# Delta rule, MLP and gated unit on one core: weight loads on another queue, other steps for the next pair's normalization

## The chip, the cores and the metric

The kernel runs on one core of a Trainium2 chip. The core's engines are TensorE (PE; its weight loads are shown as PEld), VectorE (DVE), ScalarE (ACT), GpSimd (POOL) and SyncE (SP, which here only issues DMAs). Each works through its own instructions in order and waits on semaphores for the others. The metric is the device time of one execution in microseconds, the median of several runs. Times inside an execution come from one profiled execution and count from the start of its span.

## The reference

The input is 32 sequences of 512 tokens with 256 features. Cut to what matters:

```python
def delta(x, gates_w, gates_b, lr_w, lr_b, out_w, out_b):
    q, k, v = split(x @ gates_w + gates_b, 3);  lr = x @ lr_w + lr_b
    k = k / norm(k)
    A = tril(k @ k.T, -1) + eye(T)
    u = solve_triangular(A, v, lower=True)
    return ((q @ k.T) @ (lr * u)) @ out_w + out_b

h = layernorm(x)                       # no gain, no offset
h = h + delta(layernorm(h) * dn_g + dn_b)
h = h + relu((layernorm(h) * mn_g + mn_b) @ w1 + b1) @ w2 + b2
x = x + h
n = layernorm(x)
return x + (silu(n @ w_gate.T) * (n @ w_up.T)) @ w_down.T    # integer weights times 1/127
```

## The kernel before

Sequences are worked on in 16 pairs. A sequence is four chunks of 128 tokens (partitions) by 256 features, one tile `a` of 128x1024 floats out of six. The engines' orders are the orders in which the Python program emits instructions: the schedule is written out by hand, with generators that are advanced at chosen places.

**The opening.** `load_a` puts the first sequence on SP's queue. `Gates` loads the weights of q, k, v and lr in three cuts (`CUTS`, the k part first, in its constructor; the others in `load_rest`) by `load`, four to eight DMAs a cut, and DVE and PE later fold the normalization's gain and offset into them (`fold`, `keys`, `rest`). `load_rest` also loads `out_w` and `out_b`. Then SP loads the second pair's sequences and `w1`, `w2`, and ACT's queue `b1`, `b2`, `mn_g`, `mn_b`. Only then does the program emit `normalized` of the first sequence, which needs DVE (statistics), ACT (L527, subtracting the mean with a row sum) and POOL (L415, a power for the reciprocal root), and PE's first transposes after it. All DMAs of ACT and SP share eight landing semaphores in turn; an issue that takes one over waits until the DMA that had it before has landed.

**One pair.** For pair g, whose predecessor is `old` and successor `following`, the loop emits: `middle` (the MLP of `old`, and the first steps of the triangular solve of pair g); the gated stage `gated(old)`, 84 steps of one product of a weight block and 256 columns each, two matmuls; and `values_phase` (contractions of pair g, down projections of `old`). In the gated stage, unit n of 12 takes seven steps p1 to p7; ACT copies PE's results out of PSUM (L1021, L1029, L1041), DVE adds and multiplies (L1075, L1070, L1059), POOL does further products (L1047, L1048, L1053, L1071) and the sums of the second sequence's input (L979, from step `MIX` on). Beside these the loop emits by step number i: solution steps (every third i until it is done), a store at `STORE`, loads of the following pair at `LOAD` and `TURN + 1`, the second sequence's normalization from `NORM` and its fetch at `TURN`, and from `EARLY` on the next pair's keys (`keys`: `pk`, L588) and Gram blocks (`gram`: `pg`, L617), which need the next pair's normalized sequences `ag`.

**The next pair's normalization.** `prepare(following)` runs `normalized` for both sequences of the next pair, one after the other. At i == `START` it is made a `Side`: every emitted product calls `spend(columns)`, which adds `columns * weight / cols` to what the side owes (a gated step spends 256, `keys` 1024, `gram` up to 1024), and `run` emits pieces of the generator as long as something is owed. A piece costs what it yields, 1 if it yields nothing. The pieces are: four statistics (`stats`, L409 and L410), the sums `vv`, `rr`, `nm` (L514 to L522), four activations (L527), `left`, `both`, `r2` with the first scaling (L533 to L543), three more scalings (L543), two small copies (L548, L549), four transposes of 32x32 blocks on DVE (L484), the sending of the transposed chunks to DRAM (L491, four DMAs on SP) and their fetch as `ag` (L497, SP).

```python
def run(self, cols):
    self.owed += cols * self.rate
    while self.owed > 0.0 and not self.over:
        w = next(self.gen, self)
        self.over = w is self
        self.owed -= 1.0 if w is None or self.over else w
```

The functions around the change, with the profile's line numbers:

Of the kernel before, what the change touches and what calls it, by code (L numbers as in the profile page):

```python
# [15 lines left out]
P = 128  # L16
# [6 lines left out]
def kernel(  # L23
# [40 lines left out]
    LEAD = 16  # L64
    NS = 2

    LOAD, NORM, STORE, TURN, START, MIX, EARLY = 1, 3, 8, 15, 16, 28, 56
    BEGIN = 17
    PREPARE = 13 * 1024
    INVERT = 17 * 1024  # L70
    INVERT_FIRST = 15 * 1024

# [91 lines left out]
    def by_feature(src, name, queue):  # L164
        t = const.tile([P, src.shape[0] // P], F32, tag=name, name=name)
        queue.dma_start(t, src.rearrange("(c p) -> p c", p=P))
        return t
# [24 lines left out]
    class Gates:  # L192


        def __init__(self, gw):

            self.gw = gw
            self.gb = wk.tile([1, GC], F32, tag="feat", name="gb", bufs=4)
            self.wlast = wk.tile([P, GC], F32, tag="feat", name="wlast", bufs=4)
            self.wt = [wk.tile([P, GC], F32, tag="dp", name=f"wt{f}") for f in range(NF)]  # L200
            self.load(*CUTS[0])
            self.dnb = by_feature(dn_b, "dnb", nc.sync)
            self.dng = by_feature(dn_g, "dng", nc.sync)
            self.glast = const.tile([P, 1], F32, name="glast")
            nc.sync.dma_start(self.glast, dn_g[C - 1 : C].partition_broadcast(P))
            self.put = wk.tile([P, NF, P], F32, tag="rhs", name="put", bufs=4)
            nc.gpsimd.memset(self.put, 0.0)
            nc.gpsimd.tensor_copy(self.put[:, :, LAST:P], self.dnb.unsqueeze(2))

        def load(self, lo_, hi_):  # L210
            top = min(hi_, 3 * C)
            for f in range(NF):
                nc.scalar.dma_start(
                    self.gw[f][:, lo_:top], gates_w[f * P : (f + 1) * P, lo_:top]
                )
            nc.scalar.dma_start(self.gb[:, lo_:top], gates_b[lo_:top].unsqueeze(0))
            nc.scalar.dma_start(
                self.wlast[:, lo_:top], gates_w[C - 1, lo_:top].partition_broadcast(P)
            )
            if hi_ > top:  # L220
                for f in range(NF):
                    nc.scalar.dma_start(self.gw[f][:, top:hi_], lr_w[f * P : (f + 1) * P, :])
                nc.scalar.dma_start(self.gb[:, top:hi_], lr_b.unsqueeze(0))
                nc.scalar.dma_start(
                    self.wlast[:, top:hi_], lr_w[C - 1].partition_broadcast(P)
                )

# [76 lines left out]
            nc.scalar.copy(wl, pl)  # L304

        def load_rest(self):
            self.load(*CUTS[1])
            self.load(*CUTS[2])
            self.room = wk.tile([P, NH, NF, C], F32, tag="hid", name="room")
            self.rooms = 0  # L310
            self.ow = self.scratch("ow")
            nc.scalar.dma_start(self.ow, out_w.rearrange("(c p) o -> p c o", p=P))
            self.obs = wk.tile([P, C], F32, tag="rhs", name="obs", bufs=4)
            nc.scalar.dma_start(self.obs, out_b.partition_broadcast(P))

# [86 lines left out]
    def stats(src, tag):  # L404

        st = small.tile([P, NT, nc.vector.BN_STATS_DIM], F32, tag="bnst", name=f"bnst_{tag}")
        mv = small.tile([P, NT, nc.vector.BN_AGGR_DIM], F32, tag="bnmv", name=f"bnmv_{tag}")
        for c in range(NT):
            nc.vector.bn_stats(st[:, c, :], src[:, c, :])  # L409
            nc.vector.bn_aggr(mv[:, c, :], st[:, c, :])  # L410
            yield
        return mv

    def rsqrt(dst, src):
# [92 lines left out]
    def normalized(s):  # L507

        n = s.n
        mv = yield from stats(s.a, f"a{n}")  # L510


        vv = small.tile([P, 2, NT], F32, tag="vv", name=f"vv_{n}")
        nc.vector.tensor_scalar(vv[:, 0, :], mv[:, :, 1], EPS, None, ALU.add)  # L514
        nc.vector.scalar_tensor_tensor(
            out=vv[:, 1, :], in0=vv[:, 0, :], scalar=EPS, in1=mv[:, :, 1],
            op0=ALU.mult, op1=ALU.add,
        )
        rr = small.tile([P, 2, NT], F32, tag="rr", name=f"rr_{n}")
        rsqrt(rr.rearrange("p a t -> p (a t)"), vv.rearrange("p a t -> p (a t)"))  # L520
        nm = small.tile([P, NT], F32, tag="nm", name=f"nm_{n}")
        nc.vector.tensor_scalar(nm, mv[:, :, 0], -1.0, None, ALU.mult)  # L522
        yield 8

        left = small.tile([P, NT], F32, tag="left", name=f"left_{n}")
        for c in range(NT):
            nc.scalar.activation(  # L527
                s.a[:, c, :], s.a[:, c, :], AF.Identity, bias=nm[:, c : c + 1], scale=1.0,
                accum_out=left[:, c : c + 1],
            )  # L530
            yield 2
        yield 8
        nc.vector.tensor_scalar(left, left, 1.0 / C, None, ALU.mult)  # L533

        both = small.tile([P, NT], F32, tag="both", name=f"both_{n}")
        nc.vector.tensor_tensor(both, rr[:, 0, :], rr[:, 1, :], ALU.mult)
        s.r2 = small.tile([P, 2, NT], F32, tag="r2", name=f"r2_{n}", bufs=5)
        nc.vector.tensor_tensor(
            s.r2, vv, both.unsqueeze(1).to_broadcast([P, 2, NT]), ALU.mult
        )  # L540
        s.hlast = small.tile([P, NT, 1], F32, tag="hlast", name=f"hlast_{n}", bufs=5)
        for c in range(NT):
            nc.vector.tensor_scalar(  # L543
                s.a[:, c, :], s.a[:, c, :], left[:, c : c + 1], rr[:, 0, c : c + 1],
                ALU.subtract, ALU.mult,
            )
            yield 2
        nc.vector.tensor_copy(s.hlast, s.a[:, :, C - 1 : C])  # L548
        nc.vector.tensor_copy(s.a[:, :, C - 1 : C], s.r2[:, 1, :].unsqueeze(2))  # L549
        yield  # L550
        if n // NS == 1:
            s.ag = wk.tile([P, NF, T], F32, tag="aT", name=f"ag_{n}")
        else:
            s.ag = wk.tile([P, NF, T], F32, tag="feat", name=f"ag_{n}", bufs=4)
        if n >= 2 * NS:
            t = Turn(f"a{n}")
            for c in range(NT):
                t.chunk(s.a[:, c, :], c)
                yield
            t.send()  # L560
            for _ in range(4):
                yield
            t.fetch(s.ag)
        yield
# [666 lines left out]

    whole = lambda gen: [None for _ in gen]

    def middle(old, rest, sides_, sol):

        one, two = old
        combined = iter([d.combined for d in rest[2:]])
        more = lambda *between: next(combined, lambda *b: [f() for f in b])(*between)
        step = lambda: rest and next(sol, None)
        more()  # L1240
        mlp_in(one, 0)
        step()
        norm = normed_steps(two, "m")
        next(norm)
        next(norm)
        mlp_in(one, 1)
        step()
        whole(norm)
        turned(two, "m")
        residual(one)  # L1250
        if rest:
            sides_[0].finish()
        mlp_out(one, 0, step)
        mlp_out(one, 1)
        step()
        if rest:
            normed(one, "f")
        for d in rest[:2]:
            d.store()
        more(step)  # L1260
        mlp_in(two, 0)
        residual(two)
        mlp_in(two, 1)
        if not rest:
            normed(one, "f")
        step()
        mlp_out(two, 0)
        step()
        turned(one, "f")
        whole(mixed(one))  # L1270
        mlp_out(two, 1)
        step()
        if not rest:
            next(sides_[0].gen)
            sides_[0].finish()
# [160 lines left out]
    with tc.manual_schedule(engines={  # L1436
# [24 lines left out]
            load_a(s)  # L1461
        w1s = matrix(w1, "w1s")
        w2s = matrix(w2, "w2s")
        b1s = by_feature(b1, "b1s", nc.scalar)
        b2s = const.tile([P, C], F32, name="b2s")
        nc.scalar.dma_start(b2s, b2.partition_broadcast(P))
        mng = by_feature(mn_g, "mng", nc.scalar)
        mnb = by_feature(mn_b, "mnb", nc.scalar)
        for _ in normalized(first[0]):
            pass  # L1470
        to_keys(first[0])
# [19 lines left out]
        for g in range(n_pairs):  # L1491
# [5 lines left out]
                rest = []  # L1497
            else:
                sol = solution(new)
                middle(old, rest, sides_, sol)  # L1500
                prep = None
                solved = False
                early = iter(())
# [8 lines left out]
                for i, _ in enumerate(gated(old)):  # L1512
# [6 lines left out]
                    if i == STORE:  # L1519
                        for d in rest[2:]:  # L1520
                            d.store()
                    if following and i == LOAD:
                        load_a(following[0])
                    if following and i == TURN + 1:
                        load_a(following[1])
                    if i == NORM:
# [7 lines left out]
                    if i >= MIX and i % 2 == 0:  # L1534
                        next(mix, None)
                    if i == START and following:
                        prep = Side(prepare(following), 2 * 50, PREPARE)
                for _ in sol:
                    pass
                if prep:  # L1540
# [52 lines left out]
```

## Time and profile before

| | |
|---|---|
| runs | 2088.59, 2092.3, 2093.04 us; median 2092.3 |
| profiled execution | 2088.74 us, span 2086.6 us |
| busy | PE 1983.9 us (95%), DVE 1350.9 (65%), ACT 918.3 (44%), POOL 1113.1 (53%) |
| DMA | 164.12 MB, 160.29 on SP's queue (q1), 1.71 on ACT's (q10) |
| gated stages | the first starts at 163.4 us, the others 124 to 127 us apart (the first pair 140) |

In the profile, a line `start length engine Lnn operation out<-in` is one group of instructions in the timeline, with the idle time of the engine before it and what ended it in brackets. `ACTq` and `SPq` are what the engines' sequencers issue, DMAs above all. A view of waits lists who waited for whom, with the total, the number of times and the longest. PE's busy time contains the pipelining of matmuls: two that follow each other 0.215 us apart show 0.38 us each.

### The profile page before, as it was taken

The page shows a single profiled execution, that of the slowest core. Times are in us where ns is not written, and L with a number is a line of the kernel's source. Part 1 is how long each engine was busy: PE and PEld are TensorE (multiplying, and loading weights), DVE is VectorE, ACT ScalarE, POOL GpSimd, SP SyncE. Part 2 cuts the span into 40 slices and gives each one's busy share as a digit, 9 for nine tenths or more (in the row PEclk, how much of TensorE's full clock was granted, in tenths as well). Part 3 has the DMA queues.
Part 4 walks back from the last instruction along what each step waited for, and adds up shares of the span by engine and source line. Part 5 has one row for each costly group of instructions (what it writes and reads, how often), then busy time and mean ns, then how long its engine had stood idle before and what let it go on. Part 6 is the DMA issues. An engine that isn't in the chain of part 4 may idle for free.

```text
span 2086.6 us, 31085 instructions
## 1 busy us (share of the span) xinstructions
PE 1983.9 (95%) x10286; PEld 1585.7 (76%) x10286; DVE 1350.9 (65%) x3788; ACT 918.3 (44%) x2499; POOL 1113.1 (53%) x1317
## 2 busy tenths in 40 slices
PE   5888999999999999999999999999999999999998
PEld 2566786878878787786878878787786878778887
DVE  3747484875849577484875749577584866748252
ACT  3335335353443535435353443635345353543543
POOL 2524364754645465464754646465464645546568
PEclk9799999999999999999999999999999999999999
DMA  3211132332423223232332423224142332323120
GB/s 89 64 54 28 44 103 78 81 108 60 116 64 99 82 60 108 57 105 77 80 108 61 115 64 99 82 61 121 44 130 61 86 107 60 103 64 90 51 61 21
DMA packets 248344, 164.12 MB, mean 79 GB/s; under 512 B 80849, under 2 KB 223832, under 8 KB 248184
## 3 DMA queue, kind: packets, MB, share of 16 engines
q1 hardware_dynamic: 244992, 160.29, 28.0%
q10 hardware_dynamic: 3112, 1.71, 0.3%
q8 instruction: 82, 1.34, 0.3%
q14 instruction: 78, 0.64, 0.1%
q0 software_dynamic: 80, 0.14, 0.0%
HBM read 96.02 MB, written 66.06 MB: 78 GB/s over the span
## 4 chain that ended last, share of the span: by engine, by line
PE 62%; DVE 16%; DMA 10%; ACT 4%; issue 3%; POOL 2%; SPq 2%; POOLq 0%; ACTq 0%; DVEq 0%
PE pg L617 7%; PE pk L588 5%; PE po_y L1134 5%; PE pyup L1007 5%; PE po_d L876 4%; PE pygate L1007 4%; PE pa L951 4%; PE po_x L1134 4%; PE pf L835 3%; PE pzgate L1007 3%; PE po_m L876 3%; PE pzup L1007 3%; PE pr L814 3%; DVE a L543 2%; DMA ag<-way_a 2%
## 5 line engine op out<-in xcount | busy, mean ns | idle before, releaser
L1070 DVE TENSOR_TENSOR top_up<-top_up,pzup 128x512 f32<-128x512 f32 x96 | 65.5, 682 | 223.4 <-PE pzup L1007 221.0
L1047 POOL TENSOR_TENSOR v_up<-v_up,five_up 128x256 f32<-128x256 f32 x96 | 69.9, 728 | 253.4 <-ACT v_up L1021 252.0
L1134 PEld LDWEIGHTS po_y<-wdS,hid 128*128 128x128 f32 x1536 | 179.7, 192 | 4.1 <-issue 1.0
L1134 PE MATMUL po_y<-wdS,hid 128*128 128x128 f32 x1536 | 182.8, 276 | 0.0
L1007 PE MATMUL pygate<-hS,wgS 128*128 128x256 f32 x576 | 173.7, 383 | 3.1 <-ACT top_gate L1041 2.5
L1007 PE MATMUL pyup<-hS,wuS 128*128 128x256 f32 x576 | 174.1, 384 | 1.9
L617 PE MATMUL pg<-kT 128*128 128x256 f32 (+3 forms) x512 | 159.3, 437 | 1.9 <-ACT kT L595 1.9
L1075 DVE TENSOR_TENSOR hid<-top_gate,pzgate 128x512 f32<-128x512 f32 x96 | 65.0, 677 | 143.1 <-PE pzgate L1007 143.0
L1134 PEld LDWEIGHTS po_x<-wdS,hid 128*128 128x128 f32 x1152 | 138.4, 192 | 5.4 <-POOL hid L1071 2.2
L1134 PE MATMUL po_x<-wdS,hid 128*128 128x128 f32 x1152 | 138.9, 275 | 2.0 <-POOL hid L1071 2.0
L1007 PEld LDWEIGHTS pyup<-hS,wuS 128*128 128x128 f32 x576 | 106.1, 190 | 43.1 <-issue 13.4
L1053 POOL TENSOR_TENSOR hid<-v_gate,five_gate 128x256 f32<-128x256 f32 x96 | 70.4, 733 | 127.5 <-ACT v_gate L1021 127.5
L1007 PEld LDWEIGHTS pygate<-hS,wgS 128*128 128x128 f32 x576 | 107.4, 190 | 35.5 <-issue 12.4
L588 PE MATMUL pk<-ag,wa 128*128 128x512 f32 x256 | 121.6, 599 | 7.7 <-DMA ag<-way_a 6.8
L1007 PE MATMUL pzup<-hT_f,wuS 128*128 128x256 f32 x384 | 117.9, 389 | 8.8 <-ACT five_up L1021 8.2
L876 PE MATMUL po_m<-w2s,act 128*128 128x256 f32 x512 | 125.4, 389 | 0.1
L1071 POOL TENSOR_TENSOR hid<-hid,top_up 128x512 f32<-128x512 f32 x96 | 122.6, 1277 | 0.0
L617 PEld LDWEIGHTS pg<-kT 128*128 128x128 f32 x512 | 92.7, 192 | 38.1 <-issue 10.5
L1048 POOL TENSOR_TENSOR hid<-hid,v_up 128x256 f32<-128x256 f32 x96 | 69.8, 727 | 93.1 <-ACT hid L1054 82.5
L951 PE MATMUL pa<-hT_m,w1s 128*128 128x512 f32 x256 | 116.7, 598 | 1.2 <-DVE a L943 1.2
L835 PE MATMUL pf<-a,dp 128*128 128x256 f32 x512 | 115.4, 379 | 0.0
L1007 PE MATMUL pzgate<-hT_f,wgS 128*128 128x256 f32 x384 | 115.1, 381 | 0.1
(242 smaller groups left out, 4881.7 us busy)
## 6 DMA issues: line engine op xcount, KB each, us to landing
a<-in_L_attn_x_dram SPq DMA_DIRECT2D x32, 512.0 KB, 4.9
x<-in_L_attn_x_dram SPq DMA_DIRECT2D x32, 512.0 KB, 4.1
out_dram<-a SPq DMA_DIRECT2D x64, 256.0 KB, 2.8
way_m<-turn_m SPq DMA_DIRECT2D x120, 128.0 KB, 2.3
hT_m<-way_m SPq DMA_DIRECT2D x30, 512.0 KB, 3.8
way_a<-turn_a SPq DMA_DIRECT2D x112, 128.0 KB, 2.3
ag<-way_a SPq DMA_DIRECT2D x28, 512.0 KB, 3.7
way_f<-turn_f SPq DMA_DIRECT2D x112, 128.0 KB, 2.4
```

Source lines behind the costliest of these rows:

```text
L588: nc.tensor.matmul(pk, lhsT=wa[:, f, ts(o, P)], rhs=s.ag[:, f, :], start=(f == 0), stop=(f == NF - 1),)
L617: nc.tensor.matmul(pg[:, :w], lhsT=s.kT[:, f, ts(j, P)], rhs=s.kT[:, f, j * P :], start=(f == 0), stop=(f == NF - 1),)
L835: nc.tensor.matmul(s.pp[:, o, :], lhsT=lhs[:, c, ts(o, P)], rhs=rhs[:, c, :], start=(c == 0), stop=(c == nk - 1),)
L876: nc.tensor.matmul(self.po[:, c % 2, :], lhsT=src[:, ts(c, P)], rhs=self.w[:, f, :], start=(f == 0), stop=(f == self.nk - 1),)
L951: nc.tensor.matmul(pa, lhsT=w1s[:, f, ts(o, P)], rhs=s.hT[:, f, :], start=(f == 0), stop=(f == NF - 1),)
L1007: nc.tensor.matmul(dst, lhsT=self.w[:, self.j, self.SLOT[i], :], rhs=self.s.B[i], start=first, stop=last, skip_group_check=True,)
L1047: nc.gpsimd.tensor_tensor(v, v, self.five, ALU.add)
L1048: later(5, lambda: nc.gpsimd.tensor_tensor(self.out(1, 1), self.out(1, 1), self.half(v), ALU.mult))
L1053: nc.gpsimd.tensor_tensor(to, self.half(v), self.half(self.five), ALU.add)
L1070: nc.vector.tensor_tensor(self.top, self.top, self.z, ALU.add)
L1071: later(4, lambda: nc.gpsimd.tensor_tensor(natural(g), natural(g), grouped(flat(self.top)), ALU.mult))
L1134: nc.tensor.matmul(po[:, i, :], lhsT=self.A[block][:, j, :], rhs=wdS[:, j, slot, :], start=(j == 0), stop=(j == NP - 1),)
```

## The change

Three things change. `load` takes the queue as an argument: the first cut of the weights stays on ACT's queue, and the other two cuts, `out_w`, `out_b`, `b1`, `b2`, `mn_g` and `mn_b` are issued by SP, at the same places of the program. The load of the next pair's first sequence is emitted in `middle`, before the last half of the second sequence's MLP output, and not at gated step 1; `LOAD` goes. The next pair's normalization starts at step 13, not 16 (`START`), its side has a weight of 128 over 14 x 1024 columns, not 100 over 13 x 1024, and its pieces cost other amounts: statistics 3 each (were 1), the sums 6 (8), activations 3 (2), the pause after them 4 (8), scalings 4 (2), transposes 2 (1). They add to 64 a sequence (46 before).

```diff
-    LOAD, NORM, STORE, TURN, START, MIX, EARLY = 1, 3, 8, 15, 16, 28, 56
+    NORM, STORE, START, TURN, MIX, EARLY = 3, 8, 13, 15, 28, 56
-    PREPARE = 13 * 1024
+    PREPARE = 14 * 1024
...
-            self.load(*CUTS[0])
+            self.load(*CUTS[0], nc.scalar)
...
-        def load(self, lo_, hi_):
+        def load(self, lo_, hi_, queue):
...
-                nc.scalar.dma_start(
+                queue.dma_start(
                     self.gw[f][:, lo_:top], gates_w[f * P : (f + 1) * P, lo_:top]
                 )
...
         def load_rest(self):
-            self.load(*CUTS[1])
-            self.load(*CUTS[2])
+            self.load(*CUTS[1], nc.sync)
+            self.load(*CUTS[2], nc.sync)
...
-            nc.scalar.dma_start(self.ow, out_w.rearrange("(c p) o -> p c o", p=P))
+            nc.sync.dma_start(self.ow, out_w.rearrange("(c p) o -> p c o", p=P))
...
             nc.vector.bn_aggr(mv[:, c, :], st[:, c, :])
-            yield
+            yield 3
...
         nc.vector.tensor_scalar(nm, mv[:, :, 0], -1.0, None, ALU.mult)
-        yield 8
+        yield 6
...
                 accum_out=left[:, c : c + 1],
             )
-            yield 2
-        yield 8
+            yield 3
+        yield 4
...
                 ALU.subtract, ALU.mult,
             )
-            yield 2
+            yield 4
...
                 t.chunk(s.a[:, c, :], c)
-                yield
+                yield 2
...
         whole(mixed(one))
+        if following:
+            load_a(following[0])
         mlp_out(two, 1)
...
-        b1s = by_feature(b1, "b1s", nc.scalar)
+        b1s = by_feature(b1, "b1s", nc.sync)
...
-                    if following and i == LOAD:
-                        load_a(following[0])
...
-                        prep = Side(prepare(following), 2 * 50, PREPARE)
+                        prep = Side(prepare(following), 2 * 64, PREPARE)
```

More of the change, by code (lines that the diff above doesn't have):

```diff
@@ L208, in __init__ @@
             nc.gpsimd.tensor_copy(self.put[:, :, LAST:P], self.dnb.unsqueeze(2))
-        def load(self, lo_, hi_):
+        def load(self, lo_, hi_, queue):
             top = min(hi_, 3 * C)
             for f in range(NF):
-                nc.scalar.dma_start(
+                queue.dma_start(
                     self.gw[f][:, lo_:top], gates_w[f * P : (f + 1) * P, lo_:top]
                 )
-            nc.scalar.dma_start(self.gb[:, lo_:top], gates_b[lo_:top].unsqueeze(0))
-            nc.scalar.dma_start(
+            queue.dma_start(self.gb[:, lo_:top], gates_b[lo_:top].unsqueeze(0))
+            queue.dma_start(
                 self.wlast[:, lo_:top], gates_w[C - 1, lo_:top].partition_broadcast(P)
@@ L221, in load @@
                 for f in range(NF):
-                    nc.scalar.dma_start(self.gw[f][:, top:hi_], lr_w[f * P : (f + 1) * P, :])
-                nc.scalar.dma_start(self.gb[:, top:hi_], lr_b.unsqueeze(0))
-                nc.scalar.dma_start(
+                    queue.dma_start(self.gw[f][:, top:hi_], lr_w[f * P : (f + 1) * P, :])
+                queue.dma_start(self.gb[:, top:hi_], lr_b.unsqueeze(0))
+                queue.dma_start(
                     self.wlast[:, top:hi_], lr_w[C - 1].partition_broadcast(P)
@@ L311, in load_rest @@
             self.ow = self.scratch("ow")
-            nc.scalar.dma_start(self.ow, out_w.rearrange("(c p) o -> p c o", p=P))
+            nc.sync.dma_start(self.ow, out_w.rearrange("(c p) o -> p c o", p=P))
             self.obs = wk.tile([P, C], F32, tag="rhs", name="obs", bufs=4)
-            nc.scalar.dma_start(self.obs, out_b.partition_broadcast(P))
+            nc.sync.dma_start(self.obs, out_b.partition_broadcast(P))
     NP = NH // 2
@@ L1232, with middle @@
     whole = lambda gen: [None for _ in gen]
-    def middle(old, rest, sides_, sol):
+    def middle(old, rest, sides_, sol, following):
         one, two = old
@@ L1463 @@
         w2s = matrix(w2, "w2s")
-        b1s = by_feature(b1, "b1s", nc.scalar)
+        b1s = by_feature(b1, "b1s", nc.sync)
         b2s = const.tile([P, C], F32, name="b2s")
-        nc.scalar.dma_start(b2s, b2.partition_broadcast(P))
-        mng = by_feature(mn_g, "mng", nc.scalar)
-        mnb = by_feature(mn_b, "mnb", nc.scalar)
+        nc.sync.dma_start(b2s, b2.partition_broadcast(P))
+        mng = by_feature(mn_g, "mng", nc.sync)
+        mnb = by_feature(mn_b, "mnb", nc.sync)
         for _ in normalized(first[0]):
@@ L1499 @@
                 sol = solution(new)
-                middle(old, rest, sides_, sol)
+                middle(old, rest, sides_, sol, following)
                 prep = None
```

## The prediction

> **What bounds the kernel now.** I read the page's busy shares first.
>
> ```profile
> span 2086.6 us, 31085 instructions
> PE 1983.9 (95%) x10286; PEld 1585.7 (76%) x10286; DVE 1350.9 (65%) x3788; ACT 918.3 (44%) x2499; POOL 1113.1 (53%) x1317
> PEclk9799999999999999999999999999999999999999
> ```
>
> TensorE is busy for 1983.9 of 2086.6 us at full clock from the third slice on, so only the rest, some 100 us, can be won by reordering. Where it lies I read from PE's waits (waited for: us in total, times, longest).
>
> ```profile
> PE tp_a L465 <- DVE a L543: 22.8, 1, 22.8
> PE pygate L1007 <- DVE hid L1075: 15.0, 13, 1.2
> PE pzup L1007 <- ACT five_up L1021: 8.2, 14, 0.7
> PE pk L588 <- DMA ag<-way_a: 6.8, 13, 1.0
> PE pyup L1007 <- ACT five_gate L1021: 6.5, 13, 0.5
> ```
>
> One wait of 22.8 us stands before PE's first instruction; four others come once per pair and have to do with the next pair's normalization. Third, the timeline of the first 23 us (start, length, engine, what).
>
> ```profile
> 2.25 0.36 ACTq L217 DMA_DIRECT2D wlast<-in_L_attn_gates_w_dram  x1
> ...
> 7.69 0.16 DVE L522 TENSOR_SCALAR nm<-bnmv_a 128x4 f32<-128x4 f32 x1
> 7.86 1.67 POOL L415 TENSOR_TENSOR rr<-vv,neghalf 128x8 f32<-128x8 f32 x1 [1.74 <-DVE nm L522]
> ...
> 18.06 0.48 ACTq L166 DMA_DIRECT2D mnb<-in_L_attn_mn_b_dram  x1
> 18.57 1.28 ACT L527 ACT_TABLE_LOAD   x1 [18.57 <-DMA b1s<-in_L_attn_b_dram]
> 19.87 0.51 ACT L527 ACTIVATE a<-a,nm 128x256 f32<-128x256 f32 x1
> ...
> 21.97 0.17 DVE L533 TENSOR_SCALAR left<-left 128x4 f32<-128x4 f32 x1 [14.12 <-ACT a L527]
> ...
> 22.83 2.45 PE L465 MATMUL tp_a<-ident,a 128*128 128x128 f32 x8 [22.83 <-DVE a L543]
> ```
>
> The mean that ACT's L527 needs is there at 7.69 + 0.16 = 7.85, but ACT, which works in order, is issuing DMAs until 18.54 and loads its table after that. Last, the timeline of a middle pair whose gated stage starts at 1177.6.
>
> ```profile
> 1197.76 0.39 DVE L533 TENSOR_SCALAR left<-left 128x4 f32<-128x4 f32 x1
> 1198.88 2.90 DVE L543 TENSOR_SCALAR a<-a,left,rr 128x256 f32<-128x256 f32 x3
> 1199.58 1.31 POOL L1071 TENSOR_TENSOR hid<-hid,top_up 128x512 f32<-128x512 f32 x1
> 1202.30 0.89 DVE L543 TENSOR_SCALAR a<-a,left,rr 128x256 f32<-128x256 f32 x1
> 1203.64 1.42 DVE L484 STREAM_TRANSPOSE turn_a<-a 128x256 f32<-128x256 f32 x4
> 1205.09 1.93 SPq L491 DMA_DIRECT2D way_a<-turn_a  x4
> 1208.94 0.38 SPq L497 DMA_DIRECT2D ag<-way_a  x1
> 1212.81 1.55 PE L588 MATMUL pk<-ag,wa 128*128 128x512 f32 x3 [0.48 <-DMA ag<-way_a]
> ```
>
> This is the chain that sets the first `pk`: scale (L543), transposes (L484) done at 1205.06, out, back in, and PE waits for it.
>
> **The weights on SyncE.** Of ACT's 22 opening issues 18 go. Their lengths in the timeline add to 6.95 us; the other 9 us before 18.57 were waits for landings, for each DMA after the first eight is issued only when an earlier one has landed (SP's own queue shows one of 4.2 us for `a`). After, ACT's last issue ends at 2.25 + 0.36 = 2.61, the table load (1.28) at 3.9, and L527 starts at 7.9: 19.87 - 7.9 = 11.97 us sooner. L533 also needs POOL's `rr`, done at 7.86 + 1.67 = 9.53, before the four activations end (7.9 + 2.08 = 9.98). PE's transposes move from 22.83 to 10.9. What could be late next: the key weights (landed 6.8), `dng` 5.97, `glast` 8.46, needed at 24.03 - 11.97 = 12.06; the second sequence, issued at 5.81, needed at 28.07 - 11.97 = 16.1. All are ahead on SP as before. The third sequence, which SP issued at 6.22, now stands behind 14 weights as the program's 24th DMA. The whole opening issued 31 SP and ACT DMAs from 0.74 to 18.5, so 0.6 us each by the same landings whichever engine issues; the 24th leaves at about 0.74 + 23 x 0.6 = 14.5 and lands 5 to 6.3 us later, at 19.5 to 20.8, and is wanted by DVE at 34.95 - 11.97 = 23.0. SP itself has 27 issues of some 0.4 us, 11 us, hidden by the landings. If the cover of 2 to 3.5 us went, only what is over it would be paid, in DVE's chain. `out_w`, `out_b` (wanted at 53.8 - 12 = 41.8), `w1`, `b1` and the rest are far off. SP's first dependent transfer, L635, was at 40.0 and would be at 28; SP is free by 20. I take -11.9, with PE's cold start at either end: bounds -13 and -7 (the issues alone).
>
> [...]
>
> **The earlier load of the next pair.** On SP it follows the fetch of `hT_f` (1173.11) at 1174.49 already, and the next SP instruction is at 1185.42; between its new and old places in program order (`mlp_out`, the solution's step, two gated steps) SP gets nothing. Its order does not change: nothing either way, no wait added.
>
> **The spacing.** A `Side` runs a piece when the columns spent reach its place: before 100 units over 13312 columns, 1.923 a gated step of 256, from step 17; after 128 over 14336, 2.286 a step, from step 14. Adding the yields gives each piece's step. Means and sums: stats 17 to 18, now 14 to 17; `nm` 19 in both; activations 23, 24, 25, 26, now 21, 23, 24, 25; `left` with the first L543 at 31, now 28; the other L543 at 32, 33, 34, now 30, 32, 34; L548 at 35 in both; transposes 36, 36, 37, 37, now 36, 37, 38, 38; send 38, now 39; fetch 40, now 41. A step is 0.43 us (two matmuls of 0.215), but the engines run in order and are late, so I replay the middle pair.
>
> DVE first: L1070 (to 1190.6), L1059, four stats of 0.555, two `vv` and `nm` are the same set in both orders, so `nm` still ends near 1194.1. ACT: the first activation now stands before L1063 (step 22, ran at 1193.83) and holds it until `nm` comes: L1063 slips to 1194.6, and the `pygate` of 1194.49 which takes over its PSUM tile slips about 0.55; by the `v_up` copy (1196.27) the lag is 0.65. POOL's train behind that copy (L1047 and seven more, without a gap from 1196.71 to 1203.04) starts 0.65 later, so its instructions end at 1198.1, 1198.8, 1199.6, 1200.3, 1201.5, 1202.3, 1203.0 and 1203.7.
>
> That train is what stretches DVE: of 128 L543, 73 took 0.41 us, and each of the 55 longer ones (0.79 to 1.36) ended 0.15 us after a POOL instruction ended; L538 (0.17 or 0.70) and L548 (0.17 or 0.69) go the same way, while instructions that read PSUM, stats and transposes keep their length. So each such piece uses up one POOL instruction. Before, L533, L538, four L543 caught six of the train, one of them L1071's 1.31. After, `left` runs at 1197.2, ahead of the train; L538 ends with the first POOL end, L543 with the second; L1059 0.42; L543 with the third and fourth; L1075 to 1201.1; L543 with the fifth (1201.65), L548 with the sixth, L549 with the seventh (1203.15), and the transposes take 1.42: 1204.6 against 1205.06. The way out and back was 1212.81 - 1205.06 = 7.75 us and does not change, so `pk` starts at 1212.35: -0.5 a pair. PE's other waits become shorter (L1075 ends 1201.1, not 1202.38, so the 1.16 us one goes), but PE then waits longer for `ag`; without that wait PE would be there at about 1211.0, so no more than -1.8 is to be had. The other end is one more POOL instruction caught: +0.73 - 0.5 = +0.25. I take -0.5, the replay's own value. The second sequence's `ag` (landed 1224.62, wanted 1226.7) has 2.1 us of cover; its fetch is some two steps, 0.9 us, later by program order, so hidden. Thirteen pairs have this (the second to the fourteenth): -6.5, ends -23 and +3.
>
> The first gated pair differs: there L723, which ends the inversion PE waits for (PE idle 3.4 us at 180.5), came behind two of the four stats and now comes behind all four: 2 x 0.555 = +1.1, ends 0 and +3 (with a window at half clock, as the one seen there).
>
> **Sum.** -11.9 - 6.5 + 1.1 = -17.3. The profiled execution took 2088.7 (2086.6 and 2.1 around it), so 2071.4 on its scale; the median of the runs, 2092.3, is 3.6 higher, and I forecast 2075.0 on that.
>
> **Rivals.** (1) Slower: the same lock on DVE. From the forecast, every further POOL instruction that a piece of this chain catches costs 0.73 a pair, all of it on `ag`. The opening leaves 11.9 - 1.1 = 10.8; it is spent at 10.8 / 13 = 0.83 a pair over before, 1.3 over the forecast: with two more the sum is 13 x (1.46 - 0.5) - 10.8 = +1.7, 2094; with three +11, 2104. For it: eight such pieces stand beside a train of eight, some POOL instructions are longer, and that L549 catches only one is assumed. Against: the first has moved ahead of the train, and the replay already charges both copies. (2) The train leaves a gap, since its L1053 and L1048 wait for ACT, and the pieces, further apart, fall into it at 0.41 each: -1.8 a pair to PE's own pace, -23.4 - 10.8 = -34, 2058. For it: 73 of 128 L543 met no POOL work. Against: none of the first sequence's in a middle pair did. (3) Only the issue time is won at the start, because some landing holds the fold or the third sequence 5 us: -6.95 - 6.5 + 1.1, 2080. For it: 27 issues on one queue. Against: the margins above. (4) The spacing does nothing: -10.8, 2081.5; it lies in the range of the forecast.
>
> **Chances.** The forecast, with -1.0 to 0 a pair: 0.53, own range 2067 to 2082. (1) 0.13, of which 0.05 within 0.2%; (2) 0.17; (3) 0.10; 0.07 for anything else, shared 0.04, 0.01, 0.02. Two parts in a thousand are 4.2 us, about what a measurement of this kernel tells from none. Faster 0.53 + 0.17 + 0.10 + 0.04 = 0.84, same 0.06, slower 0.10. The range 2056 to 2090 takes in the forecast, (2), (3) and some of the rest.
>
> **What would show it.** PE's first instruction near 10.9, ACT's table load near 2.6, DVE's third set of stats without a wait; the pieces at the steps above; L1075 about a microsecond sooner after the gated stage's start than the 24.1 us of before; `pk`'s wait for `ag` longer than 0.5 us while `pygate`'s for L1075 is gone; pairs of about 123.6 instead of 124.1 us. I am wrong if PE starts after 14, if a landing holds DVE in the first 40 us, or if pairs get longer than before.

## The result and the profile after

The changed kernel took 2069.99 us (median; 2069.12 to 2070.92) beside 2090.51 us for the kernel before on the same chip: 0.9901 of it, interval 0.9884 to 0.9918. The forecast was 2075.0. The profiled execution went from 2088.74 to 2069.12 us (span 2086.6 to 2067.3). The page's first lines:

```profile
span 2067.3 us, 31099 instructions
PE 1992.1 (96%) x10286; PEld 1583.0 (77%) x10286; DVE 1370.9 (66%) x3788; ACT 918.1 (44%) x2499; POOL 1113.9 (54%) x1317
```

TensorE's work is the same 10286 matmuls; the span is 19.3 us shorter. PE's waits (waited for: us in total, times, longest) show which of the five waits shown of before are left:

```profile
PE pk L588 <- DMA ag<-way_a: 12.5, 17, 1.2
PE tp_a L465 <- DVE a L543: 11.0, 1, 11.0
...
PE pygate L1007 <- DVE hid L1075: 4.4, 14, 1.2
```

The wait ahead of PE's first instruction is halved. `pygate` waits 4.4 us for L1075 in place of 15.0, and the 1.2 is a single one in the first pair; `pzup` waits for `five_up` once (0.7 us), not 14 times; `pyup`'s wait for `five_gate` is gone. In their place `pk` waits 12.5 us for `ag`, where it waited 6.8. The opening's timeline:

```profile
7.83 0.16 DVE L522 TENSOR_SCALAR nm<-bnmv_a 128x4 f32<-128x4 f32 x1
...
8.02 0.51 ACT L527 ACTIVATE a<-a,nm 128x256 f32<-128x256 f32 x1 [1.41 <-DVE nm L522]
...
10.99 2.45 PE L465 MATMUL tp_a<-ident,a 128*128 128x128 f32 x8 [10.99 <-DVE a L543]
```

ACT now stands ready when the mean is there: L522 starts at 7.83 and L527 at 8.02, where it was 7.69 and 19.87. The same stretch of a middle pair as before, whose gated stage starts at 1160.03 here:

```profile
1183.00 0.67 DVE L1075 TENSOR_TENSOR hid<-top_gate,pzgate 128x512 f32<-128x512 f32 x1
...
1185.00 0.65 DVE L549 COPY a<-r 128x4 f32<-128x4 f32 x1
...
1185.69 1.42 DVE L484 STREAM_TRANSPOSE turn_a<-a 128x256 f32<-128x256 f32 x4
...
1191.20 0.38 SPq L497 DMA_DIRECT2D ag<-way_a  x1
...
1194.90 1.55 PE L588 MATMUL pk<-ag,wa 128*128 128x512 f32 x3 [1.11 <-DMA ag<-way_a]
```

The transpositions end at 27.08 after the stage's start (27.43 in the pair shown of before), and `pk` starts at 34.87 (35.18). L1075, which stands behind three of the four L543 in both kernels, is over at 23.64 (24.75).

Where the 19.3 us of the span are: up to the first gated stage 13.1 (163.40 to 150.26), of which 11.84 by PE's first instruction (22.83 to 10.99); the first gated pair +1.6 (140.05 to 141.65); the second to the fourteenth pair 8.3 (mean 124.45 to 123.81, median 124.18 to 123.66); the fifteenth +0.8 and the end -0.3.

### The profile page after: what moved, and what is told of

Read it like the earlier page. It is cut to its first block, busy times and chain, and to the rows that moved or that the text cites. A ratio compares the mean times of both kernels' runs of the same rounds, so it can differ in the third digit from the quotient of the medians.

```text
span 2067.3 us, 31099 instructions
## 1 busy us (share of the span) xinstructions
PE 1992.1 (96%) x10286; PEld 1583.0 (77%) x10286; DVE 1370.9 (66%) x3788; ACT 918.1 (44%) x2499; POOL 1113.9 (54%) x1317
## 4 chain that ended last, share of the span: by engine, by line
PE 72%; DVE 16%; DMA 6%; ACT 2%; issue 2%; POOL 1%; SPq 1%; POOLq 0%; DVEq 0%; ACTq 0%
PE po_y L1134 6%; PE pg L617 6%; PE pyup L1007 5%; PE pk L588 5%; PE pygate L1007 5%; PE pa L951 5%; PE po_m L876 5%; PE po_d L876 4%; PE pr L814 4%; PE po_x L1134 4%; PE pzup L1007 4%; PE pf L835 4%; PE pzgate L1007 4%; DMA ag<-way_a 3%; PE pu L824 3%
## 5 line engine op out<-in xcount | busy, mean ns | idle before, releaser
L1075 DVE TENSOR_TENSOR hid<-top_gate,pzgate 128x512 f32<-128x512 f32 x96 | 65.1, 678 | 112.4 <-PE pzgate L1007 112.4
L588 PE MATMUL pk<-ag,wa 128*128 128x512 f32 x256 | 122.5, 603 | 13.6 <-DMA ag<-way_a 12.5
```

Source lines behind the costliest of these rows:

```text
L588: nc.tensor.matmul(pk, lhsT=wa[:, f, ts(o, P)], rhs=s.ag[:, f, :], start=(f == 0), stop=(f == NF - 1),)
```

## The experiments

Diffs are against the kernel before or after, as named. "Transpositions' end" is the end of the last transposition (L484) of the next pair's first sequence, counted from the start of the pair's gated stage, as the median of the second to the fourteenth pair: 27.59 us before, 27.04 after. Ratios are to the kernel before on the same chip.

### One part alone: the queue

The kernel before with the other queue, none of the rest:

```diff
-            self.load(*CUTS[0])
+            self.load(*CUTS[0], nc.scalar)
...
-            self.load(*CUTS[1])
-            self.load(*CUTS[2])
+            self.load(*CUTS[1], nc.sync)
+            self.load(*CUTS[2], nc.sync)
...
```

> The kernel before with the queue change alone. Theory (ACT's opening issues, and the landings they wait for, hold its first activation): PE starts near 11.0 us, the first gated stage 12 to 13 us sooner than 163.4, pairs as before (124.1 us); 12 to 13 us in all, a ratio of 0.994. Rival (only the issue time of the 18 moved DMAs is won): 7 us, 0.9967.

Measured: 2078.89 us, ratio 0.9958 (0.9943 to 0.9974); PE's first instruction at 10.86, the first gated stage at 149.58. The opening has the whole of the 13 us. The total shows 8: its interval holds the rival's 0.9967 and just misses the theory's 0.994, so it is the opening in the trace that decides between the two, not the total. The pairs were not as before, as was expected: the first was 141.78 (140.05 before), and the next thirteen were 4.7 us longer in all (mean 124.81, median 124.88 for 124.18). Of this 1.6 us are longer waits for `ag` (8.4 for 6.8), and the tenth pair alone took 127.19; the rest is not explained.

### One part alone: the spacing

```diff
-    LOAD, NORM, STORE, TURN, START, MIX, EARLY = 1, 3, 8, 15, 16, 28, 56
+    LOAD, NORM, STORE, START, TURN, MIX, EARLY = 1, 3, 8, 13, 15, 28, 56
-    PREPARE = 13 * 1024
+    PREPARE = 14 * 1024
...
-                        prep = Side(prepare(following), 2 * 50, PREPARE)
+                        prep = Side(prepare(following), 2 * 64, PREPARE)
```

and the yields as in the change.

> The kernel before with the spacing alone (steps, weight, yields; queues and the early load as before). Theory (the pieces run ahead of GpSimd's train of instructions, DVE's chunks are done 0.4 to 0.6 us sooner after the gated stage's start, and the keys wait for ag alone): 13 pairs shorter by 0.5 to 0.65 us, the first pair longer by 1.6: 5 to 7 us, a ratio of 0.997. Rival (the changed kernel's shorter pairs come from the earlier opening or from a disturbed pair or two of the execution of before that was profiled): no change, 1.000 or above.

Measured: 2081.61 us, ratio 0.9975 (0.9962 to 0.9987). Transpositions' end 27.01; pairs' mean 124.03, median 123.81, with one of 126.62. PE's waits here:

```profile
PE pk L588 <- DMA ag<-way_a: 13.0, 16, 2.1
...
PE pygate L1007 <- DVE hid L1075: 4.4, 14, 1.2
```

The pairs' waits are those of after, and the one before PE's first instruction (23.3 us) is that of before: the parts touch different stages. The earlier load was not run by itself; in the kernel after SP issues it 3.12 us ahead of the gated stage in the middle pair (1156.91), as it did before (3.14, 1174.49).

### What held ScalarE: issues or landings

The kernel before with only the two later weight cuts on SP; six other loads stay on ACT.

```diff
-            self.load(*CUTS[1])
-            self.load(*CUTS[2])
+            self.load(*CUTS[1], nc.sync)
+            self.load(*CUTS[2], nc.sync)
```

> The kernel before with only the two later weight cuts on SyncE's queue; out_w, out_b, b1, b2, mn_g and mn_b stay on ScalarE's. Theory: ScalarE is held by landings, not by the time its issues take; its six last issues, which take over landing semaphores of transfers issued before them, still leave at 15 to 18 us, so the mean's subtraction starts at 17 to 19 us and PE's first instruction comes at 20 to 23 us, only 0 to 3 us before the 22.83 of before; ratio 0.998 to 1.000. Rival (issue time only): 12 of the 18 moved issues are gone from ScalarE, 12/18 of 6.95 us = 4.6 us, so PE starts near 18.2 us; ratio 0.998.

Measured: 2088.16 us, ratio 0.9991 (0.9978 to 1.0003), PE's first instruction at 20.58. ACT's issues in the opening:

```profile
2.64 0.45 ACTq L312 DMA_DIRECT2D room<-in_L_attn_out_w_dram  x1
...
12.98 0.34 ACTq L314 DMA_DIRECT2D obs<-in_L_attn_out_b_dram  x1
...
16.32 1.28 ACT L527 ACT_TABLE_LOAD   x1 [16.32 <-DMA b1s<-in_L_attn_b_dram]
...
20.58 1.08 PE L465 MATMUL tp_a<-ident,a 128*128 128x128 f32 x3 [20.58 <-DVE a L543]
```

Between the issue of `out_w`, over at 3.09, and that of `out_b` at 12.98 ACT does nothing at all. A wait of this kind in the kernel before: ACT's second issue for `lr_w` left at 12.79, 0.02 us after the landing of the weight issued at 6.82 (5.95 us on its way), whose landing semaphore it takes over. Twelve issues are gone and PE starts 2.25 us sooner, half of their 4.6. So it was the waits for landing semaphores that held ACT, and the six issues left on its queue still meet them.

### The new spacing from the old step

The kernel after with the start of the pieces put back:

```diff
-    NORM, STORE, START, TURN, MIX, EARLY = 3, 8, 13, 15, 28, 56
+    NORM, STORE, TURN, START, MIX, EARLY = 3, 8, 15, 16, 28, 56
```

> The changed kernel with START put back to 16, all else as changed. Theory (it is the earlier start that lets the first scaling in ahead of GpSimd's train; the even pieces alone end later): left comes at step 31, the transposes at 39 to 41, behind L1070 of step 41, so the chunks end near 28.4 us after the gated stage's start instead of 27.1 and the first keys come at 36 instead of 34.9: 1.2 us a pair, some 15 us more than the changed kernel, a ratio to the kernel before of 0.997 to 0.999. Rival (even spacing is what counts, the start does not): as the changed kernel, 0.990.

Measured: 2121.14 us, ratio 1.0164 (1.0149 to 1.0179): slower than after, as the theory has it, but by far more than it forecast, and slower than before. The transpositions end at 28.11, 1.07 later than after and 0.3 sooner than forecast. But a pair is 127.9 us (mean), 4.1 longer. PE's waits, then three stretches around the `pk` of the fifth pair (us of the span; busy us and instructions of PE, PEld, DVE, ACT, POOL; granted clock; DMA share; GB/s):

```profile
PE pk L588 <- DMA ag<-way_a: 48.0, 23, 4.0
```

```profile
841.40:844.80 3.40, 0.00 (x0) 0.00 (x0) 0.73 (x4) 0.88 (x5) 0.31 (x1) 1.00 0.45 154
844.80:848.20 3.40, 3.19 (x4) 1.51 (x5) 0.00 (x0) 0.00 (x0) 0.00 (x0) 0.51 0.00 0
848.20:851.60 3.40, 3.40 (x12) 2.06 (x11) 2.54 (x4) 1.81 (x4) 1.93 (x2) 0.99 0.00 0
```

PE is idle through 841.4 to 844.8 and then has half the clock for 3.4 us: its first four `pk` take 3.58 us, not 1.88 as the next four. Over the whole span the granted clock was 0.977 in this execution, 0.991 in that of the kernel after. What makes the waits for `ag` longer than the 1.07 us by which the transpositions are later is not settled: from issue to landing `way_a` took 2.3 us and `ag` 3.6 (medians over both sequences), as in the kernel after.

### The old spacing from the new step

The kernel before with one number changed:

```diff
-    LOAD, NORM, STORE, TURN, START, MIX, EARLY = 1, 3, 8, 15, 16, 28, 56
+    LOAD, NORM, STORE, START, TURN, MIX, EARLY = 1, 3, 8, 13, 15, 28, 56
```

> The kernel before with START = 13 alone: three gated steps earlier, the old spacing and weights. Theory: what counts is where the scaling pieces stand against GpSimd's train and L1075; three steps earlier the scalings come at steps 28 to 31, all four of them ahead of L1075, which ends later than the 24.1 us after the stage's start of before, so PE's wait for L1075 (1.2 us there) becomes 1.5 to 2.5 us; the chain itself ends sooner or as soon. Pairs of 124.2 to 125.5 us, the first pair 141.6; ratio 1.000 to 1.008. Rival (an earlier start alone is what helps): pk's wait for ag shrinks by up to 1.3 us and pairs become 123.5; ratio 0.996 to 0.997.

Measured: 2124.53 us, ratio 1.0175 (1.0157 to 1.0193), pairs of 127.3 us (mean). PE's waits:

```profile
PE pyup L1007 <- ACT a L527: 35.4, 13, 2.7
...
PE pzgate L1007 <- DVE hid L1075: 14.4, 13, 1.5
```

The wait expected, for L1075 behind all four scalings (and two transpositions), is there, 0.7 to 1.5 us a pair. The larger one was not expected: 2.7 us in each pair, in which ACT, in order, stands at the second sequence's first L527 until DVE has its mean, while PE waits for ACT's next copy out of PSUM. The granted clock was 0.977 over the span here too, 0.991 in the kernel before. Two more expectations failed: the transpositions end at 28.35, later than before and not sooner, and the first pair took 139.15 us, not 141.6. So each half of the spacing alone, the start or the pieces' costs, leaves the kernel 1.6 to 1.8% slower than before (the run with the pieces' costs even with the shorter opening in it); only the two together gain.

### Less GpSimd work beside the chain

The kernel after with the sums of the second sequence's input (L979) six steps sooner:

```diff
-    NORM, STORE, START, TURN, MIX, EARLY = 3, 8, 13, 15, 28, 56
+    NORM, STORE, START, TURN, MIX, EARLY = 3, 8, 13, 15, 22, 56
```

> The changed kernel with MIX at 22 instead of 28: the four sums L979 of the second sequence are emitted at steps 22, 24, 26 and 28, so that two of them run in GpSimd's idle time before the train. Theory (each scaling or small copy of the first sequence uses up one GpSimd instruction of an unbroken train): the train is two instructions shorter, the last copies run free, the chunks end 0.4 us sooner and the first keys with them: 13 x 0.4 = 5 us less than the changed kernel, a ratio to the kernel before of 0.988. Rival (DVE's own work sets the chunk's end, GpSimd's place does not matter): as the changed kernel, 0.990.

Measured: 2063.8 us, ratio 0.9887 (0.987 to 0.9904); transpositions' end 26.51, pairs' mean 123.45, median 123.28. The end of the chain on DVE in the middle pair (gated stage from 1158.0):

```profile
1182.23 0.57 DVE L548 COPY hlast<-a 128x4 f32<-128x4 f32 x1
1182.84 0.17 DVE L549 COPY a<-r 128x4 f32<-128x4 f32 x1
```

Two L979 now run before POOL's train, which ends sooner. L549 meets none of it and takes 0.17 us, not the 0.65 it took in the kernel after: the half microsecond by which the transpositions are earlier. So it is in all thirteen pairs; L548 is still held (0.57). The total's interval also holds the rival's 0.990, and it is these rows that decide.

### The wait behind GpSimd by itself: a small copy against a large transposition

The kernel after with one more DVE instruction ahead of L548, in the first sequence of each next pair. The copy:

```diff
+        if n >= 2 * NS and n % NS == 0:
+            nc.vector.tensor_copy(s.hlast, s.a[:, :, C - 1 : C])
         nc.vector.tensor_copy(s.hlast, s.a[:, :, C - 1 : C])
```

> The kernel after with the small copy L548 (128x4 floats) emitted twice in a row for the first sequence of each next pair, from the second pair on. Theory (a small DVE piece beside GpSimd's train ends 0.15 us after a GpSimd instruction ends, whatever its size): the extra copy uses up one more GpSimd instruction of 0.7 to 0.8 us, so the last transposition of that sequence ends 0.6 to 0.8 us later, 27.6 to 27.8 us after the gated stage's start for 27.04, and a pair is at least 0.6 us longer. Rival (a copy costs its own 0.16 us): 27.2, pairs +0.15.

Measured: 2079.11 us, ratio 0.9967 (0.9957 to 0.9978); transpositions' end 27.78, 0.74 later than after; pairs' mean 124.70, 0.89 longer. The transposition:

```diff
+        if n >= 2 * NS and n % NS == 0:
+            t = Turn(f"a{n}")
+            t.chunk(s.a[:, 0, :], 0)
         nc.vector.tensor_copy(s.hlast, s.a[:, :, C - 1 : C])
...
-            t = Turn(f"a{n}")
+            if n % NS:
+                t = Turn(f"a{n}")
```

> The kernel after with the transposition of the first chunk (128x256 floats, L484, 64 times the copy's data) emitted once more at the same place, ahead of L548. Theory (transpositions keep their length of 0.40 us beside GpSimd, and L548 behind it would have waited for a GpSimd instruction's end anyway): the last transposition ends 0 to 0.2 us later, 27.05 to 27.25 us, pairs 0 to +0.2. Rival (it costs its own length): 27.45, pairs +0.4; with the same lock as the copy 27.7.

Measured: 2070.95 us, ratio 0.9926 (0.9906 to 0.9945); transpositions' end 27.06, 0.02 later; pairs' mean 123.86. DVE in a middle pair with the copy (lines are numbered two higher here from L548 on, with the extra copy at L549):

```profile
1193.39 0.57 DVE L549 COPY hlast<-a 128x4 f32<-128x4 f32 x1
1193.99 0.65 DVE L550 COPY hlast<-a 128x4 f32<-128x4 f32 x1
```

and with the transposition (three higher):

```profile
1184.85 0.43 DVE L484 STREAM_TRANSPOSE turn_a<-a 128x256 f32<-128x256 f32 x1
1185.21 0.33 DVE L551 COPY hlast<-a 128x4 f32<-128x4 f32 x1
```

The copies of 128x4 take 0.57 and 0.65 us, each until a POOL instruction is over. The transposition of 64 times as much takes 0.43 and the copy behind it 0.33: both go into the time in which the copy would have waited anyway. What a piece costs here is the POOL instruction that it uses up, not its own work.

### The first gated pair

The kernel after with the pieces of the first pair alone started later:

```diff
-                    if i == START and following:
+                    if i == (START if rest else START + 6) and following:
```

> The kernel after with the first pair's START at 19, every other pair's at 13. Theory of the prediction: the first gated pair is longer because four statistics stand ahead of L723; at step 19 they stand behind it and the pair falls from 141.65 to 140.0 us: 1.6 us less than after, ratio 0.989. Rival: the queue change alone, with the old steps, also had 141.78 us here, so the 1.6 us come from the clock windows that moved with the opening, and the pair stays at 141.3 to 141.9; ratio 0.990.

Measured: 2070.1 us, ratio 0.9916 (0.9902 to 0.9929). DVE in the first gated stage of after (from 150.26), and of this kernel (from 150.18):

```profile
166.66 0.42 DVE L723 COPY xc<-beside 128x256 f32<-128x256 f32 x1
```

```profile
164.78 0.42 DVE L723 COPY xc<-beside 128x256 f32<-128x256 f32 x1
```

The four statistics (L409) start at 162.41 to 165.66 in the first and at 166.01 to 167.62 in the second. With them behind it L723 comes 1.8 us sooner after the stage's start, PE's wait for the inversion ends at 20.1 and not 21.9 us after the stage's start, and the pair is 138.91 us, 2.7 less. The total does not show it: in this execution one pair (the ninth, 127.79) had a late `ag`, a wait of 2.5 us, and took 4.2 us more than in the kernel after. So a gain in this pair is shown, and one in the total is not. Nor is the order of the statistics the only thing in the first pair: the queue alone, with the old steps, had 141.78, and there the granted clock from 140 to 160 us was 0.74, 0.83 in the kernel after. That alone does not make a pair long either, for it was 0.75 in this run.

### A version that takes up what was found

The kernel after with `MIX` at 22, the first pair's later start, and the next pair's keys two gated steps later, so that PE has work while `ag` is on its way:

```diff
-    NORM, STORE, START, TURN, MIX, EARLY = 3, 8, 13, 15, 28, 56
+    NORM, STORE, START, TURN, MIX, EARLY = 3, 8, 13, 15, 22, 58
...
-                    if i == START and following:
+                    if i == (START if rest else START + 6) and following:
```

> The kernel after with MIX = 22 (as in the run above), EARLY = 58 (the next pair's keys two gated steps later, so that PE works on while ag lands) and the first pair's START at 19 for 13. Theory: -0.5 us a pair as MIX alone gave, and pk's wait for ag, near 1 us a pair, filled with two steps of 0.43 us: -0.8 a pair more; the first pair 140.0 for 141.6. In all 2070 - 6 - 10 - 1.6 = 2052 to 2056; ratio 0.982 to 0.985. Rival (another wait takes its place, since the gated steps left for later are fewer): no more than MIX alone, ratio 0.988 to 0.989.

Measured: 2052.32 us, ratio 0.9828 (0.9815 to 0.9842), against 0.9901 for the change. PE's waits:

```profile
PE tp_a L465 <- DVE a L543: 11.0, 1, 11.0
PE po_d L876 <- DVE m L859: 10.1, 19, 1.1
...
PE pk L588 <- DMA ag<-way_a: 1.9, 2, 1.0
```

`pk` waits for `ag` in two pairs only, 1.9 us in all. The pairs are 122.9 us (mean), 1.5 less than before; the replay had given 1.8 as all that PE's own pace left. A new wait, for DVE's L859 (10.1 us, no single one over 1.1), takes a part of it. That the total met its forecast is partly luck: a pair is 0.9 us shorter than in the kernel after, not 1.3, and the first pair 3.6 (138.09), not 1.6.

## Why the prediction was right, and where it was not

**The opening: right, for its reason.** Forecast -11.9 at PE's first instruction, measured -11.84. That landings held ACT, and not the 6.95 us of issues, is shown by the run with two thirds of the issues gone, which brought 2.25 us. The issue time alone, as rival (3) has it, gave 2080 and is too small here: 6.95 us for the 11.84 measured. PE's slow start, which the bounds take in, is the same in both kernels: the first eight L465 take 2.45 us, the next eight 1.04. Another 1.3 us up to the first gated stage was not in the sum: a stretch of 3.4 us at half clock, at 33.9 before, is not there after. From PE's first instruction to the stage it took 140.57 us before and 139.27 after. This part is put down to chance and not to the change: the run of the old spacing from the new step has the opening of before, and its granted clock from 20 to 50 us was 1.00, where that of the kernel before was 0.94.

**Two steps of the opening were off and cost nothing.** ACT's table load was to come at 2.6 and came at 5.33, since it waits for the first sequence to land (its releaser in the profile); it was over at 6.61, still before the mean at 7.99. The third sequence was to leave at 14.5 and left at 13.30.

**The load: nothing to be seen, as forecast.** SP issues it at the same place of the stage, but no run has it by itself.

**The spacing: right in mechanism and size.** Forecast for the middle pair: transpositions done at 27.0 after the stage's start, L1075 at 23.5, `pk` at 34.75; measured 27.08, 23.64 and 34.87. L538, the L543, L548 and L549 caught the POOL instructions that the replay gave them. Per pair -0.5 was forecast; the median fell by 0.52, the mean by 0.64, since the kernel before had two long pairs (125.92 and 126.56) in its profiled execution and the one after has none. That makes -8.3 for -6.5, and the surplus is chance too. The run with the spacing alone excludes rival (4), the one with the queue alone rival (3). The price in rival (1), 0.73 for one more POOL instruction caught, was measured as 0.74, and 0.89 a pair.

**The first gated pair: the term was too small, and its cause is open in part.** Forecast +1.1, measured +1.6: L723 starts 1.54 us later after the stage's start (14.87 to 16.41) and PE's wait for the inversion ends 1.4 later. Two statistics are 1.1 us; the rest of L723's delay was not taken apart. The clock has a part as well. L723 before, and then the stretches at half clock behind that wait, one before and two after (columns as in the run of the new spacing):

```profile
178.27 0.39 DVE L723 COPY xc<-beside 128x256 f32<-128x256 f32 x1
```

```profile
184.13:187.54 3.41, 3.41 (x21) 2.93 (x20) 1.66 (x4) 0.00 (x0) 0.72 (x1) 0.50 0.00 0
```

```profile
171.27:174.68 3.41, 2.54 (x18) 2.33 (x19) 2.90 (x9) 0.00 (x0) 1.81 (x3) 0.50 0.14 22
174.68:178.09 3.41, 3.41 (x17) 2.49 (x16) 1.75 (x4) 0.37 (x1) 0.00 (x0) 0.50 0.03 5
```

The second stretch at half clock costs some 1.7 us by estimate, half of its 3.41. In the run of the old spacing from the new step L723 came nearly as late (16.26), the granted clock from 160 to 200 us was 0.94 (0.91 both before and after), and the pair took 139.15 us, less than before. How much of the 1.6 is the statistics' and how much the clock's is not settled.

**The sum.** Forecast -17.3 on the span, measured -19.3: opening 1.2, pairs 1.8 better, first pair and end 1.0 worse. Most of what is better is the chance named above (1.3 and 1.6 us). Beside the kernel before on the same chip, 2090.51 - 17.3 = 2073.2 was to be expected, 2069.99 came.

**What the expectations missed.** The two runs of half the spacing were to differ from the kernel before by under 1% and were 1.6 and 1.8% slower. Pairs 4.1 us longer than after and 2.9 longer than before have, by estimate, 2.3 us each of the clock in them (0.977 for 0.991 of the span, over 13 pairs), and longer waits for the rest. The prediction adds PE's waits up; only in its bound for the first pair does the clock enter. By the price of its rival (1) the start at 16, with transpositions 1.07 us later, would have cost 13 x 1.07 = 14 us over the kernel after; the spans differ by 51. The rival did not come about, but at 1.07 us it was priced too low.

## What to carry to other kernels

An engine that computes should not issue transfers ahead of its first work when landing semaphores are shared: here it was not the issues that cost, but each wait for a landing, and six late issues left on the engine kept 9.6 of the 11.84 us. Where small DVE pieces run beside a dense stretch of GpSimd work, count GpSimd instructions, not DVE time (the copy of 128x4 cost 0.74 us here, the transposition of 128x256 0.02): move pieces ahead of the stretch, or thin it out. A PE wait of 3.99 us for `ag` had 3.4 us at half clock behind it (the new spacing from the old step), so a wait like it is worth filling with other work while the transfer is on its way. A shorter wait need not be worth its full length: in the last version a wait near 0.9 us was filled (13.1 us in all with `MIX` at 22 alone, 1.9 here), and a pair was 0.5 us shorter than with `MIX` at 22 alone.

## What the runs showed of the hardware that was not expected

**Half clock behind long idle times of PE.** In the traces of the kernels before and after, the stretches at half clock begin on one grid of 3.41 us and last 3.41, 6.83 or 17.07 us (the last one runs to the end). From 120 us to 60 us before the end, four intervals of this grid with PE idle for 2.41 to 3.41 us had half clock in the next one or two: those from 153.41 and 180.72 before (idle 3.41 and 3.18) and from 140.55 and 167.86 after (3.41 and 2.41). So had the one from 841.4 in the run of the new spacing from the old step (3.40). In the other intervals at full clock of the two traces PE was idle for 1.67 us at most, and none had half clock behind it. Among them are the two into which the wait of 2.31 us in the first pair of after falls (153.28 to 155.59), with 0.93 and 1.38 us of idle time. Single pairs were 2.3 to 4 us longer than their median in the runs of the queue, the spacing and the first pair (127.19, 126.62 and 127.79, longest waits for `ag` 1.5, 2.1 and 2.5 us); what part the clock had in them is not shown.

**Which DVE instructions were held beside GpSimd.** The copies L548 and L549, the scalings by columns (L543) and L538, a product of two SBUF operands, ended just behind a GpSimd instruction where they were longer: L538 took 0.70 and not 0.17 us and ended 0.02 after it, L549 0.65 and not 0.17, ending 0.03 after it, and 55 of the 128 L543 of before took 0.79 to 1.36 and not 0.41, ending 0.15 after it. Transpositions (L484, 0.40 to 0.45 us), statistics (L409, 0.38 to 0.43) and L1059, which has an operand in PSUM (0.38 to 0.42), took no longer beside GpSimd. The pair of runs with the copy and the transposition agrees: 0.74 against 0.02 us.
